# Splitting the product S4 B22 of a tile pair into seven quarter products in matrices four to seven of a relational graph layer

## The chip, the cores and the metric

The kernel runs on one core of one Trainium2 chip. The metric is the device time of one execution in microseconds (us); the kernel before took 1364.59, 1365.10 and 1367.09 us in three runs, a median of 1365.1 us. The profile is of one further execution.

A core has five engines that run side by side, each in the order of its own instructions, and wait for each other by semaphores: TensorE (PE in the profile, its weight loads PEld), VectorE (DVE), ScalarE (ACT), GpSimd (POOL) and SyncE (SP, which here only issues transfers). TensorE writes to PSUM, eight banks of 128 partitions x 512 fp32 values; DVE and ACT read them.

## The reference

All arrays are fp32. N = 1250 nodes, D = 1024 features, R = 8 relations, E = 20000 edges sorted by destination.

```
h = relu(layernorm(x))
u = h @ root + bias
for r in range(8):
    sums = segment_sum(h[src] * (edge_type == r), dst)       # one row for each node
    u   += (sums / max(count of such edges, 1)) @ weight[r]
z   = concat([u, x']) @ w_gate + b_gate                      # x' is the layer's input, h
out = x + tanh(u) * z + h * (1 - z)
```

## The kernel before

**Order of the arithmetic.** The kernel multiplies first and gathers afterwards: y_r = h @ weight[r] for every relation, then for each node the weighted sum of rows of y. So there are eleven matrices of 1024 x 1024 (`NM`): eight relations (numbers 0 to 7), the root (8) and the two halves of w_gate (9 and 10). `step(s, i, ...)` multiplies matrix s by row tiles i and i + 5 (2 x 128 rows) of h. Ten row tiles make five steps i = 0 to 4 a matrix.

**One step.** `product` takes the two row tiles as the upper and lower half of a left matrix, halves it in columns too, and halves the right matrix both ways (blocks of 512 x 512). It forms the result by Winograd's variant of Strassen's scheme: seven products of blocks where eight would be needed. The left sums S1 to S4 are kept for all matrices in `h_op`, the right sums T1 to T4 (`make_t1` and so on) are made by DVE for each matrix. Every block product is four matmuls of 128 x 512 (`add`). The order is A11, S1 (T1), S2 (T2), S3 (T3), S4 (B22), A22 (T4), with A12 (B21) apart; two banks, b and c, collect sums. ACT copies partial results into the output rows (lines 331, 338, 342, 360) or into a tile `part` (317), and DVE adds the rest (310, 318, 326). After each block product `done()` calls `between(j)`, j = 0 to 6, where work for DVE, POOL and the queues is put in.

**Pairs.** In matrices 1 to 9 the steps (0, 1) and (2, 3) are pairs (`paired`). Their two products A12 B21, which share the right block, are taken together, by the same scheme one level lower: class `Second` makes seven products of quarters, each of two matmuls of 128 x 256 (line 213). They are hung between the block products of the two steps by the dictionary `fill`, under the names "first" to "fourth" of the place after which they stand. The result row `to` of the even step's first tile is kept until the odd step has added its share (lines 240, 241, 244), and is then stored (`put(i - 1, 0, to)`); the odd step's share is added in lines 247, 248 and 251.

**PSUM.** Six of the eight banks rotate under the name `ps` (`bank()`); two more, `ps_n` and `ps_q`, have one buffer each and serve the index work in matrices 0 to 3. A tile's next use waits until the readers of the one before are through.

**Edges.** The index work of the first matrices sorts edges into slots for each node. From matrix 4 on, `edges(g, ...)` gathers rows of y by POOL transfers into four buffers `got` (line 1065), and DVE adds each, scaled, to a sum `u` (lines 1071, 1073): group 0 beside matrices 4 and 5, group 1 beside 6 and 7, group 2 beside 8 and 9. `spread` deals these out over the calls of `between`, about one gather a block product. Matrix 10 and the gate come last. Everything is ordered by hand (`manual_schedule`): the text of the program is the order on each engine.

**Other names that the change touches.** `key_col`, `row_col` and `rank` hold three columns of numbers for the edges; they are kept to the end, because a branch for overlong edge lists (`tc.If(passes > 0)`), which this input doesn't take, reads them again. `bias_bc` is the bias spread over the partitions (read at line 398 from matrix 8 on), `t_w` and `far_k` are small scratch tiles of the edge weights and of `passes_needed`.

Of the kernel before, what the change touches and what calls it, by code (L numbers as in the profile page):

```python
# [19 lines left out]
def tile_rgcn_highway(  # L20
# [95 lines left out]
    table_more = dram.tile([G * KEYS * MORE, 1], I32, name="table_more")  # L116
    val_dram = dram.tile([G, KEYS], F32, name="val_dram")
# [134 lines left out]

    def transposed(aop, part, of, n, relu=False):


        for half, to in enumerate(((A11, A12), (A21, A22))[part]):
            p = bank().rearrange("p (k f) -> p k f", k=KQ)
            for i in range(KQ):
                k = KQ * half + i
                nc.tensor.transpose(p[:, i, :n], of[:n, k * P:(k + 1) * P], ident[:n, :n])  # L260
            to_n, p_n = aop[:, to, :, :n], p[:, :, :n]
            if half and relu:
                nc.vector.tensor_scalar_max(to_n, p_n, 0.0)
            elif half:
                nc.vector.tensor_copy(to_n, p_n)
            else:
                nc.scalar.activation(to_n, p_n, AF.Relu if relu else AF.Copy)
            if n < P:
                nc.gpsimd.memset(aop[:, to, :, n:], 0.0)
# [9 lines left out]
    def product(aop, w, to, between=lambda j: None, last=None, pieces=1, whole=True,  # L279
                fill=None, second=None, third=None):  # L280
# [48 lines left out]
        b, c = bank(), bank()  # L329
# [15 lines left out]
        if whole and not third:  # L345
            p3()
            d = p7()
            if not second:
                p2()
        else:  # L350
            d = p7()
            if third:
                last(d, 0)
            p3()
# [26 lines left out]
    waiting = {}  # L381

    def step(s, i, between=lambda j: None, second=None):
# [21 lines left out]
        def beside(j):  # L405
# [3 lines left out]
            if two and i == 0:  # L409
                sums(j)  # L410
            if two and (i, j) == (1, 6):
                Second(fac[s], 2).left()
# [26 lines left out]
        fill = {}  # L439
        if two:  # L440
            e, to = waiting[i - i % 2]
            if i == 0:
                fill = dict(sixth=lambda: (e.second(), e.second_to_first(to)))
            elif i == 1:
                fill = dict(first=lambda: e.first(),
                            fifth=lambda: (e.sixth(), True),
                            sixth=lambda: (e.seventh(), e.to_first(to), 0)[-1],
                            seventh=lambda: (e.fourth(), e.to_second(t[0]), put(i - 1, 0, to),
                                             0)[-1],
# [6 lines left out]
            else:  # L456
                fill = dict(first=lambda: (e.to_second(t[0]), e.fourth_to_second(t[0]), 0)[-1],
                            sixth=lambda: (e.second(), True),
                            seventh=lambda: (e.second_to_first(to), put(i - 1, 0, to), 0)[-1])
        product(h_op[i], fac[s], t, between=beside, whole=not two, fill=fill, second=second)  # L460
# [13 lines left out]
    key_col = const.tile([P, NCH], F32, name="key_col")  # L474
    row_col = const.tile([P, NCH], I32, name="row_col")
    rank = const.tile([P, NCH], F32, name="rank")
# [70 lines left out]
    with ExitStack() as early:  # L547
# [148 lines left out]
        tb_col = ix1.tile([P, NCH], F32, name="tb_col")  # L696
        less_lo = ix1.tile([P, NCH], F32, name="less_lo")
# [319 lines left out]
        def index():  # L1017
            for _ in zip_longest(norms(), columns()):
                yield
            with tc.tile_pool(name="ix", bufs=2) as ix:  # L1020
                yield from slots(ix)
            yield from order()
# [17 lines left out]
    with ExitStack() as edges_part:  # L1040
        gpool = edges_part.enter_context(tc.tile_pool(name="gpool", bufs=GOT))
        upool = edges_part.enter_context(tc.tile_pool(name="upool", bufs=UB))
        bias_bc = edges_part.enter_context(tc.tile_pool(name="bpool", bufs=1)).tile(
            [P, D], F32, name="bias_bc")
        nc.sync.dma_start(bias_bc, bias[None, :].to_broadcast([P, D]))
        small = edges_part.enter_context(tc.tile_pool(name="small", bufs=1))
        t_w = small.tile([P, ND, SLOTS], F32, name="t_w")
        drc = small.tile([P, ND], F32, name="drc")

        def weights(g):  # L1050
            slot_weights(g, idx[:, g, :, :SLOTS], w_of[:, g], t_w, drc)
# [3 lines left out]
        def got():  # L1055
# [4 lines left out]
            return t  # L1060

# [71 lines left out]
        def passes_needed():  # L1133

            far_k = small.tile([P, NHI], F32, name="far_k")
# [72 lines left out]
        with tc.If(passes > 0):  # L1208
# [22 lines left out]
            done = rank  # L1231
            nc.vector.tensor_single_scalar(done, rank, float(-SLOTS), op=OP.add)
# [30 lines left out]

        LG = G - 1
# [186 lines left out]
```

## Time and profile before

| what | value |
|---|---|
| three runs, us | 1364.59, 1365.10, 1367.09 |
| the profiled execution, us | 1364.05 |
| its span from first to last instruction, us | 1362.3 |
| mean granted TensorE clock | 0.999 |
| matmul records of 128 x 512 (line 293) | 2784, mean 594 ns with overlap |
| matmul records of 128 x 256 (line 213) | 504, mean 380 ns with overlap |
| DVE waiting for gathers, matrices 4 to 7, us | 103.4 |
| POOL waiting for DVE, matrices 4 to 7, us | 120.7 |
| HBM read and written, MB | 214.20 and 80.65 |

How to read it: busy time of an engine is the union of its instructions; for PE, whose matmuls overlap, the mean of one is longer than its share of the time. A row of the timeline gives start, duration, engine, line of the kernel, operation, output <- inputs, shape and count; in square brackets stand the idle time of the engine before it and what ended that. A fp32 matmul of the program leaves two records on PE. Line numbers are those of the kernel before.

### The profile page before, as it was taken

How to read it: one execution, taken by the hardware profiler on the slowest of the kernel's cores; microseconds unless marked ns; L12 is line 12 of the kernel's file. 1: busy time of each engine (PE TensorE's matmuls, PEld its weight loads, DVE VectorE, ACT ScalarE, POOL GpSimd, SP SyncE). 2: the span in 40 equal slices, each digit the busy share in tenths (PEclk: the TensorE clock that was granted, in tenths of full speed). 3: DMA queues.
4: the chain of work that ended last, by engine and by line, in shares of the span. 5: the costliest groups of instructions: out<-in, count | busy, mean ns of one | idle time of the engine just before them, and what ended most of it. 6: DMA issues, size and time to landing. Idle time of an engine off the chain costs nothing.

```text
span 1362.3 us, 12814 instructions
## 1 busy us (share of the span) xinstructions
PE 1350.3 (99%) x3810; PEld 659.9 (48%) x3810; DVE 932.0 (68%) x1849; ACT 365.4 (27%) x792; POOL 639.8 (47%) x571
## 2 busy tenths in 40 slices
PE   9999999999999999999999999999999999999998
PEld 5444445455445544544554454455445445544443
DVE  7855976887884976557565746865564585568975
ACT  3235656565641111111111111111111111121220
POOL 0001655665553358657774435465443243435631
PEclk9999999999999999999999999999999999999999
DMA  8744665944663258479788628787965764587851
GB/s 308 271 182 145 95 138 141 212 85 118 158 181 95 49 172 183 109 272 225 227 286 318 223 72 294 263 289 272 342 222 195 235 226 153 190 285 244 287 188 58
DMA packets 110218, 272.77 MB, mean 200 GB/s; under 512 B 25972, under 2 KB 28002, under 8 KB 110016
## 3 DMA queue, kind: packets, MB, share of 16 engines
q0 software_dynamic: 48912, 128.60, 29.7%
q1 hardware_dynamic: 45104, 111.34, 27.2%
q10 hardware_dynamic: 16128, 31.98, 7.6%
q8 instruction: 30, 0.49, 0.2%
q14 instruction: 44, 0.36, 0.1%
HBM read 214.20 MB, written 80.65 MB: 216 GB/s over the span
## 4 chain that ended last, share of the span: by engine, by line
PE 90%; issue 4%; DVE 2%; DMA 2%; POOL 1%; SPq 1%; ACT 0%; POOLq 0%; DVEq 0%; ACTq 0%
PE ps L293 80%; PE ps L213 8%; DMA xt<-in_x_dram 1%; PE ps L260 1%; DMA w<-in_L_gnn_weight_dram 1%; PE ps_n L805 1%; POOL out_dram L497 1%; SPq L561 0%; PE ps_q L856 0%; DVE u L1276 0%; POOL got L491 0%; DVE h_op L276 0%; DVE row L1377 0%; DVE h_op L1323 0%; DVE h_op L1340 0%
## 5 line engine op out<-in xcount | busy, mean ns | idle before, releaser
L293 PE MATMUL ps<-w,h_op 128*128 128x512 f32 x2800 | 1224.4, 593 | 2.0 <-ACT row L342 1.0
L293 PEld LDWEIGHTS ps<-w,h_op 128*128 128x128 f32 x2800 | 526.5, 190 | 615.6 <-issue 600.6
L1065 POOL DMA_INDIRECT got<-y,idx x202 | 259.8, 1286 | 243.7 <-DVE u L1073 189.6
L1073 DVE SCALAR_TENSOR_TENSOR u<-got,w_of,u 128x1024 f32<-128x1024 f32 (+1 forms) x192 | 245.9, 1282 | 137.6 <-DMA got<-y,idx 135.4
L884 POOL DMA_INDIRECT table<-row_col,at_i x157 | 176.6, 1125 | 160.9 <-DVE at_i L880 74.5
L318 DVE TENSOR_TENSOR row<-row,part 128x512 f32<-128x512 f32 x55 | 37.9, 689 | 103.6 <-ACT part L317 99.8
L360 ACT COPY row<-ps 128x512 f32<-128x512 f32 x50 | 29.3, 585 | 240.5 <-PE ps L293 236.6
L317 ACT COPY part<-ps 128x512 f32<-128x512 f32 x55 | 32.2, 586 | 178.3 <-PE ps L293 164.4
L310 DVE TENSOR_TENSOR row<-row,ps 128x512 f32<-128x512 f32 x54 | 36.9, 684 | 62.3 <-PE ps L293 50.1
L331 ACT COPY row<-ps 128x512 f32<-128x512 f32 x55 | 32.2, 585 | 165.3 <-PE ps L293 154.7
L338 ACT COPY row<-ps 128x512 f32<-128x512 f32 x55 | 32.2, 586 | 146.2 <-PE ps L293 131.4
L213 PE MATMUL ps<-w,w 128*128 128x256 f32 x288 | 71.3, 380 | 0.0
L342 ACT COPY row<-ps 128x512 f32<-128x512 f32 x55 | 32.2, 586 | 139.0 <-PE ps L293 133.3
L213 PEld LDWEIGHTS ps<-w,w 128*128 128x128 f32 x288 | 54.4, 190 | 20.9 <-issue 15.3
L528 POOL DMA_INDIRECT node_dram<-ids,pos_i x30 | 40.1, 1336 | 45.4 <-issue 45.4
L870 DVE SCALAR_TENSOR_TENSOR junk<-k_bc,key_col,before 128x128 f32<-128x128 int32 x157 | 54.9, 350 | 4.2
L810 DVE TENSOR_TENSOR seen<-seen,ps_n 128x110 f32<-128x110 f32 x157 | 42.1, 268 | 21.1 <-PE ps_n L805 11.8
L213 PE MATMUL ps<-w,h_op 128*128 128x256 f32 x216 | 56.0, 382 | 0.0
L213 PEld LDWEIGHTS ps<-w,h_op 128*128 128x128 f32 x216 | 40.5, 190 | 25.6 <-issue 22.1
L787 ACT ACTIVATE is_lo<-io,less_lo 128x128 bf16<-128x128 f32 x157 | 50.1, 391 | 0.7 <-DMA xh_dram<-xt 0.7
L938 DVE SCALAR_TENSOR_TENSOR junk<-v_bc,val,one 128x1280 bf16<-128x1280 f32 x30 | 46.5, 1550 | 0.8
L491 POOL DMA_INDIRECT u<-u_dram,node x20 | 22.5, 1126 | 51.3 <-DMA last_dram<-u 35.0
(187 smaller groups left out, 957.7 us busy)
## 6 DMA issues: line engine op xcount, KB each, us to landing
y<-row SPq DMA_DIRECT2D x72, 512.0 KB
w<-in_L_gnn_weight_dram ACTq DMA_DIRECT2D x21, 1024.0 KB
w<-in_L_gnn_weight_dram SPq DMA_DIRECT2D x10, 1024.0 KB
k_bc<-keys_dram SPq DMA_DIRECT2D x39, 256.0 KB
l_bc<-los_dram SPq DMA_DIRECT2D x39, 256.0 KB
w<-in_L_gnn_w_gate_dram ACTq DMA_DIRECT2D x6, 1024.0 KB
h_dram<-h_op SPq DMA_DIRECT2D x9, 512.0 KB
hr_dram<-row SPq DMA_DIRECT2D x9, 512.0 KB
```

The lines of the kernel that those rows point to most:

```text
L213: nc.tensor.matmul(p, a[:, k, :], b[:, k, :], start=(fresh and k == 0), stop=(k == 1), skip_group_check=True)
L293: nc.tensor.matmul(b[:, at], aop[:, i, k, :], w.of[i][:, k, at], start=(fresh and k == 0), stop=(k == KQ - 1), skip_group_check=True)
L310: nc.vector.tensor_add(c12, c12, c)
L318: nc.vector.tensor_add(c22, c22, d)
L528: ins = nc.gpsimd.indirect_dma_start(out=node_dram[g][:, :], out_offset=bass.IndirectOffsetOnAxis(ap=pos_i[:, g, d:d + 1], axis=0), in_=id ...
L787: nc.scalar.activation(is_lo[:, i, :], io, AF.Abs, bias=less_lo[:, c0 + i:c0 + i + 1])
L810: nc.vector.tensor_add(seen[j][:, i, :], was, p[:, i, :])
L870: nc.vector.scalar_tensor_tensor(junk, o["k_bc"][:, i, :], key_col[:, c:c + 1], before, op0=OP.is_equal, op1=OP.mult, accum_out=rank[:, c: ...
L884: ins = nc.gpsimd.indirect_dma_start(out=table[:, :], out_offset=bass.IndirectOffsetOnAxis(ap=at_i[:n, i:i + 1], axis=0), in_=row_col[:n, ...
L938: nc.vector.scalar_tensor_tensor(junk, v_bc[:, g, :], val[:, c:c + 1], one.to_broadcast([P, KEYS]), op0=OP.is_gt, op1=OP.mult, accum_out=p ...
L1065: nc.gpsimd.indirect_dma_start(out=t[:n], out_offset=None, in_=y[g][:, :], in_offset=bass.IndirectOffsetOnAxis(ap=at[:n, d, k:k + 1], axis=0),
L1073: nc.vector.scalar_tensor_tensor(u[:n], t[:n], w, u[:n], op0=OP.mult, op1=OP.add)
```

## The change

In matrices 4 to 7 (`thirds(s)`: R0[1] < s < ROOT, with R0[1] = 3 and ROOT = 8) the two products S4 B22 of a pair are also taken together as seven products of quarters, in a new class `Third`. Its sums s1, s2, t1, t2 are made in two goes in four small tiles (`room`), the second go (`next_sums`) writing over the first. Three of the seven products are added to what already stands in PSUM: in the even step bank c, which holds S1 T1, is now the tile `ps_n` (`hold`) and is kept until the odd step; the odd step's c and the tile `ps_q` take the others. The odd step's "first" place gets three quarter products (`first`), the place of S4 B22 gets one in the even step (`second`) and three in the odd one (`last`). The row `to` is stored after `last_to`, no longer at the place "seventh".

To make room in memory, the three edge columns move to the index pool and are written to DRAM by three transfers on SP between `slots` and `order`, the untaken branch reads them back, `t_w` and `far_k` become gather buffers, and `bias_bc` is loaded after the branch instead of at the start of the edge part.

```diff
+    edges_dram = dram.tile([3, P, NCH], F32, name="edges_dram")
...
+    class Third:
+        def __init__(self, f, i, room):
+            b = f.place["b22"]
+            self.b11, self.b12, self.b21, self.b22 = [
+                b[:, k:k + 2, c:c + H] for k in (0, 2) for c in (0, H)]
+            self.a11, self.a12, self.a21, self.a22 = [
+                h_op[i + o][:, S4, k:k + 2] for o in (0, 1) for k in (0, 2)]
+            self.t1, self.t2, self.s1, self.s2 = room
+        def sums(self):
+            nc.vector.tensor_add(self.s1, self.a21, self.a22)
+            nc.vector.tensor_sub(self.t1, self.b12, self.b11)
+            nc.vector.tensor_sub(self.s2, self.s1, self.a11)
+            nc.vector.tensor_sub(self.t2, self.b22, self.t1)
+        def next_sums(self):
+            nc.vector.tensor_sub(self.s1, self.a11, self.a21)
+            nc.vector.tensor_sub(self.t1, self.b22, self.b12)
+            nc.vector.tensor_sub(self.s2, self.a12, self.s2)
+            nc.vector.tensor_sub(self.t2, self.b21, self.t2)
+        def hold(self):
+            self.c0 = psum.tile([P, CG, P], F32, name="ps_n", bufs=1).rearrange("p c k -> p (c k)")
+            return self.c0
+        def second(self, c):
+            Second.add(self, c[:, :H], self.a12, self.b21)
+        def first(self):
+            self.b = psum.tile([P, 512], F32, name="ps_q", bufs=1)[:, :H]
+            self.c = bank()[:, :H]
+            self.p = rows.tile([P, Q], F32, name="part", bufs=2)
+            Second.add(self, self.b, self.a11, self.b11, True)
+            nc.scalar.copy(self.p[:, :H], self.b)
+            Second.add(self, self.c, self.s1, self.t1, True)
+            Second.add(self, self.b, self.s2, self.t2)
+            nc.scalar.copy(self.p[:, H:], self.b)
+        def last(self, c):
+            Second.add(self, self.b, self.s1, self.t1)
+            Second.add(self, self.c0[:, H:], self.s2, self.b22)
+            Second.add(self, c[:, :H], self.a22, self.t2)
+        def first_to(self, to):
+            nc.vector.tensor_add(to, to, self.p)
+            nc.vector.tensor_add(to[:, H:], to[:, H:], self.c)
+        def fifth_to(self, to):
+            nc.vector.tensor_add(to[:, H:], to[:, H:], self.c)
+        def last_to(self, to, to1, c):
+            nc.vector.tensor_add(to, to, self.c0)
+            nc.vector.tensor_add(to1, to1, c)
+            nc.vector.tensor_add(to1.rearrange("p (a n) -> p a n", a=2),
+                                 to1.rearrange("p (a n) -> p a n", a=2),
+                                 self.b[:, None, :].to_broadcast([P, 2, H]))
...
-        b, c = bank(), bank()
+        b = bank()
+        c = inner.hold() if inner and inner.holds else bank()
...
-            p3()
+            if inner:
+                inner.then(c)
+                done()
+                filled("third")
+            else:
+                p3()
...
+    def thirds(s):
+        return R0[1] < s < ROOT
...
+            if q and i % 2 == 0 and j == 1:
+                q.sums()
+            if q and i % 2 and j == 1:
+                q.next_sums()
+                q.first_to(to[:, Q:])
+            if q and i % 2 and j == 4:
+                q.fifth_to(t[0][:, Q:])
...
+                def then(c):
+                    if q.holds:
+                        q.second(c)
+                    else:
+                        q.last(c)
+                        q.last_to(to[:, Q:], t[0][:, Q:], c)
+                        put(i - 1, 0, to)
...
-                fill = dict(first=lambda: e.first(),
+                fill = dict(first=lambda: (e.first(), q and q.first(), 0)[-1],
...
-                            seventh=lambda: (e.fourth(), e.to_second(t[0]), put(i - 1, 0, to),
-                                             0)[-1],
+                            seventh=lambda: (e.fourth(), e.to_second(t[0]),
+                                             q or put(i - 1, 0, to), 0)[-1],
...
-                fill = dict(first=lambda: (e.to_second(t[0]), e.fourth_to_second(t[0]), 0)[-1],
+                fill = dict(first=lambda: (e.to_second(t[0]), e.fourth_to_second(t[0]),
+                                           q and q.first(), 0)[-1],
...
+            for k, t in enumerate((key_col, row_col.bitcast(F32), rank)):
+                nc.sync.dma_start(edges_dram[k], t)
             yield from order()
...
-        bias_bc = edges_part.enter_context(tc.tile_pool(name="bpool", bufs=1)).tile(
-            [P, D], F32, name="bias_bc")
-        nc.sync.dma_start(bias_bc, bias[None, :].to_broadcast([P, D]))
...
+        inner_pool = inner_part.enter_context(tc.tile_pool(name="inner", bufs=1))
+        room = [inner_pool.tile([P, 2, n], F32, name=f"inner{k}")
+                for k, n in enumerate((H, H, P, P))]
...
+            t_w = got()[:, :ND * SLOTS].rearrange("p (d k) -> p d k", k=SLOTS)
...
-            far_k = small.tile([P, NHI], F32, name="far_k")
+            far_k = got()[:, :NHI]
...
+        inner_part.close()
+        bias_bc = edges_part.enter_context(tc.tile_pool(name="bpool", bufs=1)).tile(
+            [P, D], F32, name="bias_bc")
+        nc.sync.dma_start(bias_bc, bias[None, :].to_broadcast([P, D]))
```

## The prediction

> **What bounds the kernel now.** I read three views in this order. First the page's table of engines:
>
> ```profile
> PE 1350.3 (99%) x3810; PEld 659.9 (48%) x3810; DVE 932.0 (68%) x1849; ACT 365.4 (27%) x792; POOL 639.8 (47%) x571
> ```
>
> TensorE (PE) is busy for 1350.3 of 1362.3 us. A busy PE need not be a PE at its peak, and an average says nothing of the stage that is changed. So second, the busy time by stretches; each is one matrix long (four, five, six and seven), cut where the last product of the matrix before ends:
>
> ```profile
> 514.20:633.00 118.80, 118.80 (x306) 57.54 (x305) 67.24 (x85) 17.63 (x33) 81.26 (x72) 1.00 0.76 203
> 633.00:751.70 118.70, 118.70 (x305) 57.48 (x304) 77.55 (x88) 17.63 (x33) 75.51 (x68) 1.00 0.82 261
> 751.70:870.70 119.00, 119.00 (x307) 57.60 (x306) 74.01 (x111) 17.63 (x33) 53.46 (x47) 1.00 0.63 223
> 870.70:989.40 118.70, 118.70 (x305) 57.51 (x304) 76.73 (x80) 17.63 (x33) 63.92 (x58) 1.00 0.80 280
> ```
>
> After the stretch and its length come PE, weight load, VectorE (DVE), ScalarE (ACT), GpSimd (POOL), granted clock, DMA share. PE equals the length in all four, at clock 1.00: matmul records set the time, and a record less or shorter counts in full. DVE is idle for 41 to 52 us of each. The list of waits over these stretches says what for: 103.4 us in all on gathers (DMA got<-y), 39.4 on ACT's part, 16.6 on PE. Third, what one record costs. PE in order of time, in matrix five, tile pair 1:
>
> ```profile
> 657.94 1.03 PE L213 MATMUL ps<-w,h_op 128*128 128x256 f32 x4
> 658.81 1.03 PE L213 MATMUL ps<-w,w 128*128 128x256 f32 x4
> 659.67 3.60 PE L293 MATMUL ps<-w,h_op 128*128 128x512 f32 x8
> 663.10 1.89 PE L213 MATMUL ps<-w,w 128*128 128x256 f32 x8
> 664.83 3.60 PE L293 MATMUL ps<-w,h_op 128*128 128x512 f32 x8
> 668.26 1.03 PE L213 MATMUL ps<-w,w 128*128 128x256 f32 x4
> 669.13 3.67 PE L293 MATMUL ps<-w,h_op 128*128 128x512 f32 x8
> 672.64 1.03 PE L213 MATMUL ps<-w,h_op 128*128 128x256 f32 x4
> ```
>
> A product of four matmuls leaves eight records, two for each. The second column holds the tail that overlaps the next line, so the price is the distance of the starts: 663.10 - 659.67 = 3.43 us for 8 wide records, 0.429 each; 664.83 - 663.10 = 1.73 for 8 narrow ones, 0.216 each.
>
> **The part on PE.** In each of two pairs of four matrices the two S4 products (2 x 4 matmuls, 16 wide records) go: 16 x 0.429 = 6.86 us. Seven quarter products of two matmuls come, 28 narrow records: 28 x 0.21625 = 6.06 us. That is 0.80 a pair, and **6.4 us** over eight pairs.
>
> A rule that speaks against it: the Trainium skill, "TensorE: Matmul & The Clock Gate", section "Back-to-back issue gap", has a stream of weight loads and matmuls sustain 81 ns a matmul at 128 columns and 131 ns at 512. On a straight line that is an estimated 98 ns at 256, so 0.75 of the wide price. By it 28 records would cost 28 x 0.75 x 0.429 = 9.0 us, a loss of 2.1 a pair and 17 us in all. The rows above give 0.50, because the load (190 ns in the groups by shape) fits under a 216 ns record. The row decides; twenty narrow records in a row, which the change makes, are not in the trace, but the x8 line has no slope within it.
>
> **New cover problem on ACT.** In an even product the S3 result in b is copied by ACT (L317), and the last product adds onto b afterwards. The S4 product lay between, 3.43 us; in the pair's even product now two quarter matmuls, 0.86 us. That case is in the trace: at 668.26 four narrow records stand between S2 and the S3 that needs the copy L342. PE then takes 672.64 - 668.26 = 4.38 us where 0.86 + 3.43 = 4.29 would do, 0.09 lost. It recurs in product 0 of each matrix (product 2 keeps four more matmuls there): 4 x 0.09 = **0.4 us** lost. In first(), b is rewritten after 0.86 us too, but its copy is a 256-wide one of 0.37 us (L219) that starts 0.2 us after its records end, 0.29 us before it is needed: 0.
>
> **DVE.** Per pair, from the rows: sums and next_sums each 2 x 0.69 (as L203) + 2 x 0.42 (as L206 to L209) = 2.22; first_to 0.69 + 0.42; fifth_to 0.42; last_to 3 x 0.68 (as L310); less two L310. 4.44 + 1.11 + 0.42 + 2.04 - 1.36 = 6.65 us a pair, 13.3 a matrix. The last addition of last_to reads a 256-wide bank twice over, for which there is no row: between 0.41 (256 elements written) and 2 x 0.41; L310 has its written size, so 0.68. DVE goes from 67-78 to 81-91 us of 117: not the bound, and hidden in the mean by those waits for gathers. What counts is being late. DVE runs strictly in order, and here it is late already, in matrix five, behind a gather:
>
> ```profile
> 677.17 1.28 DVE L1073 SCALAR_TENSOR_TENSOR u<-got,w_of,u 128x1024 f32<-128x1024 f32 x1 [5.51 <-DMA got<-y,idx]
> 678.37 0.68 DVE L240 TENSOR_TENSOR row<-row,w 128x512 f32<-128x512 f32 x1
> 679.16 0.42 DVE L241 TENSOR_TENSOR row<-row,ps 128x256 f32<-128x256 f32 x1
> 679.50 0.69 DVE L318 TENSOR_TENSOR row<-row,part 128x512 f32<-128x512 f32 x1
> 680.10 1.28 DVE L1073 SCALAR_TENSOR_TENSOR u<-got,w_of,u 128x1024 f32<-128x1024 f32 x1
> 681.29 0.42 DVE L247 TENSOR_TENSOR row<-row,w 128x256 f32<-128x256 f32 x1
> 681.75 0.42 DVE L248 TENSOR_TENSOR row<-row,w 128x256 f32<-128x256 f32 x1
> 682.09 0.68 DVE L310 TENSOR_TENSOR row<-row,ps 128x512 f32<-128x512 f32 x1
> ```
>
> The S4 product that L310 adds ended at about 676.9 on PE, so DVE is 5.2 us behind. Until now nobody waited: its bank came back six banks later. After the change that place holds last_to, and its first addition frees c0, the single ps_n bank, which product 2 needs for S1. So the **new wait** is PE's, for DVE, two products after last(). Behind it stands the whole PE stream. Worked out: the gather that lands at 677.17 was issued at 672.80 by POOL, which was held up by its own idx and node gathers and did not wait for DVE; so next_sums, first_to and sums disappear in the waits before it (4.3, 5.5 us and five of about 0.8 us in this pair). Behind it only fifth_to is new, 0.34 to the next start: the first addition runs 682.43 to 683.11. S1 of product 2 starts at 683.80 now; it comes earlier by 1.5 (matrix four) and 0.7 (this pair), at 681.6. PE would stand for 1.5 us.
>
> It may be more. The gathers may come later, for POOL waits for DVE to free a buffer (120.7 us here), and the Trainium skill, "GPSIMD Engine Reference", section "Specifications", says that GpSimd's SBUF interfaces contend with DVE instructions that have two SBUF inputs; 5 of the 6.65 us are of that kind. The row L1065 runs from 984 to 5668 ns, median 1013, mean 1286, so issues do stretch, though the row does not say why. By the median alone 1.5 stands; if the two sums (4.4 us) were half pushed into the gather it would be near 4. It may be nothing, if the gather lands 1.6 us sooner. I take **2 us**, near the row, with ends 0 and 4. Matrix four has 2.5 us to spare by the same sum (L310 at 560.79, S1 of product 2 at 565.05); in six and seven L310 waits for PE, so DVE is not behind there. The second pair's c0 has product 4 in between: no wait.
>
> **What costs nothing, and its cover.** PE's wait for next_sums: they stand at product 1's second step, four PE stages (about 7 us or more) before last(); without that cover, DVE's lag would be paid here first. The even tile's row store moves from the fourth quarter product to behind last_to; SP then holds this pair's other stores behind it, and ACT's copy into that row (S1 of product 2) would wait, about 10 us after last() ends; a late copy would delay S3 some 5 us further on. ACT gets two 0.37 us copies a pair in an engine busy 18 of 119. The edge columns go out by three SP issues (0.3 to 0.4 us each, as L912) at about 426 us, ahead of val_dram, v_bc, the rc stores and y stores: up to 1.2 us on a queue whose readers come steps later. The bias load moves from 515 us to behind the register read at 990.7 on SP; its first reader is L398 at 1012.5, 21 us of cover. t_w and far_k take gather buffers: one POOL memset (0.98) ahead of the first gather, at 508 us, whose reader comes at 522. The edges_dram reads on POOL lie in the branch that isn't taken.
>
> **Sum.** -6.4 + 0.4 + 2.0 = -4.0 us. On the profiled execution (span 1362.3, whole 1364.05, so 1.75 around it) that is 1360.0; the median of the runs stands 1.05 above it, so 1365.1 - 4.0 = **1361.1**.
>
> **Rivals.** (A) Likeliest, 0.45: one stand in matrix five, 1360.0 to 1362.3. (B) All is hidden, 0.25: DVE's idle 41 us speak for it, the 5.2 us lag against; 1365.1 - 6.0 = 1359.1. (C) The change doesn't do what it says in time, 0.17: stands in several first pairs, say 1.4 us in each of four matrices, eat the gain: -6.0 + 5.6 gives 1364.7. Against it is L310's wait for PE in six and seven. (D) Slower, 0.13: the ps_n handover, after the first pair of every matrix. If the added 13.3 us push gathers and lag together so that each first pair stands as at matrix five's upper end, 4 us: 16 - 6 = +10, 1375. It decides from 2.2 us a matrix on (8.7 in all). For it: POOL and DVE wait for each other already; against it: DVE idles a third of each matrix.
>
> **Range and chances.** A measurement of this kernel can tell about 0.2% (2.7 us) from no change. B starts at 1358.6 with a little room for the rows' rounding; C reaches 1367.5, and only D's upper part and a strip of C lie outside: 1358.6 to 1367. A's own range is 1360.0 to 1362.3. Faster (under 1362.4): A and B, less a little for A's upper end: 0.68. Same: C and that bit: 0.18. Slower: D and C's end: 0.14.
>
> **What would show it.** L293's wide records fall by 8 x 16 = 128 and narrow L213 ones rise by 8 x 28 = 224. Right: matrices four, six and seven some 1.5 us shorter, five less, with a PE wait for DVE before the S1 of its product 2. Wrong: runs of narrow records at more than 0.22 us each (the rule), PE waits for s1 or t1 at last(), a stand in every matrix (D), or ACT standing for a row store.

## The result, and the profile after

The changed kernel takes 1359.91 us (median of 22 runs, 1358.51 to 1367.83); the kernel before, beside it, 1365.20 us (22 runs, 1364.29 to 1367.09). The ratio is 0.9967, with a 95% interval of 0.9959 to 0.9975: faster by 4.5 us, between 3.4 and 5.6. The ratio is one of means; the medians lie 5.3 us apart. Eighteen of the 22 runs lie from 1358.5 to 1361.7, with a median of 1359.4, four from 1364.2 to 1367.8; that tail comes up again below. The profiled execution took 1361.69 us, the longest of the eighteen; it has a span of 1359.9 us at a granted clock of 0.999.

The page's table of engines, after:

```profile
PE 1344.6 (99%) x3906; PEld 677.5 (50%) x3906; DVE 976.3 (72%) x1945; ACT 371.3 (27%) x808; POOL 648.9 (48%) x571
```

PE has 96 records more (224 narrow ones come, 128 wide ones go) and 5.7 us less of busy time. The stretches of matrices four to seven, after, cut as before:

```profile
515.80:633.00 117.20, 117.20 (x330) 61.98 (x329) 78.02 (x109) 19.09 (x37) 81.25 (x71) 1.00 0.71 195
633.00:752.40 119.40, 117.43 (x329) 61.89 (x328) 88.78 (x112) 19.10 (x37) 80.58 (x69) 1.00 0.85 264
752.40:869.80 117.40, 117.40 (x331) 62.08 (x330) 85.32 (x135) 19.09 (x37) 56.12 (x47) 1.00 0.65 227
869.80:987.00 117.20, 117.20 (x329) 61.98 (x328) 87.71 (x104) 19.10 (x37) 64.14 (x58) 1.00 0.82 284
```

Three matrices are 1.5 to 1.6 us shorter than before and PE is busy all through them. Matrix five is 0.7 us longer, and its PE column is 1.97 us short of its length: one wait. The list of waits, after, names it first:

```profile
PE ps_n L356 <- DVE row L309: 2.0, 1, 2.0
```

And in order of time, matrix five, PE:

```profile
672.76 1.03 PE L214 MATMUL ps<-w,h_op 128*128 128x256 f32 x4
673.62 1.03 PE L214 MATMUL ps_q<-inner,inner 128*128 128x256 f32 x4
674.49 1.03 PE L214 MATMUL ps_n<-w,inner 128*128 128x256 f32 x4
675.35 1.03 PE L214 MATMUL ps<-inner,h_op 128*128 128x256 f32 x4
676.22 7.03 PE L356 MATMUL ps<-w,h_op 128*128 128x512 f32 x16
685.22 3.70 PE L356 MATMUL ps_n<-w,h_op 128*128 128x512 f32 x8 [1.97 <-DVE row L309]
```

Lines 673.62 to 675.35 are `last()`: four narrow records each 0.865 us from the next, 0.216 a record, as priced. (Twenty in a row stand from 655.48 to 659.79 us, again 0.216 each.) Then come 16 wide ones, and S1 of product 2 stands 1.97 us for the single `ps_n` bank. DVE in the same window:

```profile
679.23 1.28 DVE L1175 SCALAR_TENSOR_TENSOR u<-got,w_of,u 128x1024 f32<-128x1024 f32 x1 [2.82 <-DMA got<-y,idx]
...
682.16 0.41 DVE L306 TENSOR_TENSOR row<-row,ps 128x256 f32<-128x256 f32 x1
...
684.48 0.68 DVE L309 TENSOR_TENSOR row<-row,ps_n 128x512 f32<-128x512 f32 x1
```

The gather that held DVE landed at 679.23, 2.06 us later than before, when matrix four had begun 1.6 us later; behind it `fifth_to` (L306) and `last_to` (L309) follow in order.

Below, a matrix's length is the distance between the starts of ACT's last copy at line 429 (the last copy of a step) in two successive matrices. Before: 118.76, 118.76, 118.98, 118.76 for matrices four to seven. After: 117.19, 119.43, 117.41, 117.20, a sum 4.03 less.

### The profile page after: what moved, and what is told of

The parts are those of the page before. It is cut to its first block, busy times and chain, and to the rows that moved or that the text cites. A ratio compares the mean times of both kernels' runs of the same rounds, so it can differ in the third digit from the quotient of the medians.

```text
span 1359.9 us, 13144 instructions
## 1 busy us (share of the span) xinstructions
PE 1344.6 (99%) x3906; PEld 677.5 (50%) x3906; DVE 976.3 (72%) x1945; ACT 371.3 (27%) x808; POOL 648.9 (48%) x571
## 4 chain that ended last, share of the span: by engine, by line
PE 45%; DMA 6%; issue 5%; DVE 4%; POOL 2%; POOLq 0%; DVEq 0%
PE ps L356 37%; DMA got<-y,idx 5%; PE ps L214 5%; PE ps_n L356 1%; DVE u L1175 1%; PE ps_q L214 1%; POOL got L1167 1%; DMA node_dram<-ids,pos_i 1%; PE ps_n L214 1%; POOL out_dram L593 1%; PE ps L322 0%; DVE w L204 0%; POOL idx L587 0%; DVE w L181 0%; POOL got L587 0%
## 5 line engine op out<-in xcount | busy, mean ns | idle before, releaser
L356 PE MATMUL ps<-w,h_op 128*128 128x512 f32 x2608 | 1145.1, 593 | 3.0 <-issue 1.2
L356 PEld LDWEIGHTS ps<-w,h_op 128*128 128x128 f32 x2608 | 489.7, 190 | 568.8 <-issue 553.4
L1167 POOL DMA_INDIRECT got<-y,idx x202 | 264.8, 1311 | 231.7 <-DVE u L1175 173.7
L429 ACT COPY row<-ps 128x512 f32<-128x512 f32 x50 | 29.2, 584 | 222.6 <-PE ps L356 204.9
L395 ACT COPY row<-ps 128x512 f32<-128x512 f32 x55 | 32.1, 585 | 163.0 <-PE ps L356 149.7
L406 ACT COPY row<-ps 128x512 f32<-128x512 f32 x55 | 32.2, 585 | 138.6 <-PE ps L356 132.1
L402 ACT COPY row<-ps 128x512 f32<-128x512 f32 x47 | 27.5, 585 | 127.9 <-PE ps L356 106.9
L373 DVE TENSOR_TENSOR row<-row,ps 128x512 f32<-128x512 f32 x38 | 26.0, 685 | 44.8 <-PE ps L356 29.8
L214 PEld LDWEIGHTS ps<-w,h_op 128*128 128x128 f32 x216 | 40.5, 190 | 25.6 <-issue 22.3
```

Of the source, the lines that this page charges most:

```text
L214: nc.tensor.matmul(p, a[:, k, :], b[:, k, :], start=(fresh and k == 0), stop=(k == 1), skip_group_check=True)
L356: nc.tensor.matmul(b[:, at], aop[:, i, k, :], w.of[i][:, k, at], start=(fresh and k == 0), stop=(k == KQ - 1), skip_group_check=True)
L1167: nc.gpsimd.indirect_dma_start(out=t[:n], out_offset=None, in_=y[g][:, :], in_offset=bass.IndirectOffsetOnAxis(ap=at[:n, d, k:k + 1], axis=0),
```

## The experiments

The theory on trial at the outset: PE gains 1.57 us a matrix, DVE's new work is hidden, the moves of buffers and transfers cost nothing, and matrix five loses 2.2 us because DVE comes late from a gather and TensorE needs the single bank. Its rivals: the moves or DVE's work cost time by themselves; the stand comes from the sums that the change puts on DVE; the lateness has other ways to TensorE than that bank.

The experiments ran in four batches, each on another chip, and the kernel before has another median in each (1361.8 to 1365.9 us). So each ratio is taken against the runs of before in the same batch, and within a profile the lengths of matrices are compared. The first four matrices drift too: matrix four starts at 511.9 to 519.1 us over the profiles, at 514.27 in the one of before, 512.82 in a second one, 515.86 in the one of after. The last column of the table is from one profiled execution of each kernel, which need not be a usual one: that of `no_sums` (1366.81 us) is the longest of its twelve, those of `second_pairs` (1366.19) and `five_first_pair` (1366.42) are 3 us above their medians.

| kernel | us, median (lowest to highest, runs) | ratio to before (95%) | matrices four to seven, us |
|---|---|---|---|
| the change | 1359.91 (1358.51 to 1367.83, 22) | 0.9967 (0.9959 to 0.9975) | 117.19, 119.43, 117.41, 117.20 |
| moves_only | 1364.62 (1363.59 to 1368.74, 11) | 1.0008 (1.0000 to 1.0017) | 118.76, 118.76, 118.98, 118.76 |
| dve_only | 1367.90 (1363.71 to 1375.41, 11) | 1.0030 (1.0011 to 1.0048) | 118.76, 118.76, 118.98, 118.76 |
| no_sums | 1360.82 (1358.23 to 1366.81, 12) | 0.9979 (0.9969 to 0.9989) | 117.19, 123.91, 117.41, 117.19 |
| act_c0 | 1368.47 (1366.70 to 1369.89, 5) | 1.0033 (1.0020 to 1.0046) | 117.19, 124.35, 117.41, 117.20 |
| second_pairs | 1363.17 (1358.41 to 1367.24, 12) | 1.0000 (0.9987 to 1.0013) | 117.93, 124.57, 118.15, 117.94 |
| skip_five | 1358.59 (1357.12 to 1360.75, 7) | 0.9969 (0.9959 to 0.9980) | 117.19, 118.76, 117.41, 117.19 |
| later_group | 1364.34 (1361.91 to 1371.50, 12) | 1.0015 (1.0003 to 1.0028) | 118.42, 117.19, 123.16, 117.42 |
| spread_groups | 1369.60 (1368.31 to 1371.97, 5) | 1.0055 (1.0041 to 1.0069) | 117.19, 117.19, 124.35, 117.41 |
| five_first_pair | 1363.33 (1360.13 to 1371.52, 12) | 0.9984 (0.9967 to 1.0001) | 117.90, 122.30, 117.41, 117.19 |
| before_again | 1362.60 (1) | | 118.76, 118.76, 118.98, 118.76 |
| dve_again | 1361.75 (1) | | 118.76, 118.81, 118.98, 118.76 |
| after_again | 1362.79 (1) | | 117.19, 123.68, 117.41, 117.19 |

### The moves alone, and the kernel before once more

`moves_only` keeps every move of buffers and transfers and takes the new products nowhere:

```diff
     def thirds(s):
-        return R0[1] < s < ROOT
+        return False
```

> All moves of the change (edge columns by way of DRAM, t_w and far_k in gather buffers, bias loaded later, the four room tiles) and none of the quarter products. Theory (they are hidden): the time of before within 0.1%, 1364 to 1366.5. Rival (the 1.6 us by which matrices 0 to 3 ended later in the profile of the changed kernel come from the moves): 1366.7, and the start of matrix four in the profile at 515.9 us instead of 514.3.

> The kernel before, profiled once more. If the first four matrices vary by themselves, matrix four starts 1.5 us or more away from the 514.3 us of the first profile; if the moves of the change cost what the profiles with them show (start at 515.9 to 519.1), it starts at 513.8 to 514.8 again, and matrices four to seven take 118.8 each.

The ratio is 1.0008, and the four matrices have their old lengths to 0.01 us. But matrix four starts at 516.76 us in this profile, even later than the rival said. The start varies with the batch, though, and this batch has no profile of before. In the batch that has one (512.82 us), two kernels with all the moves, `skip_five` and `second_pairs` below, start matrix four at 512.41 and 512.99. So the moves cost nothing that these runs can tell (up to 0.0017 of the time, 2.3 us, is within the interval), and the 1.6 us by which matrix four starts later in the profile of after is most likely drift.

### DVE's work alone

`dve_only` takes TensorE's products as before and keeps additions of the same shapes beside them on DVE, into tiles that nothing reads:

```diff
...
+            if inner and not inner.holds:
+                nc.vector.tensor_add(inner.t2, inner.t2, inner.t2)
+            p3()
...
-                q.first_to(to[:, Q:])
+                nc.vector.tensor_add(q.s1, q.s1, q.s1)
+                nc.vector.tensor_add(q.t1, q.t1, q.t1)
...
-                q.fifth_to(t[0][:, Q:])
+                nc.vector.tensor_add(q.s2, q.s2, q.s2)
```

> The kernel with both S4 products as before on PE, but with DVE's added work: sums and next_sums as they are, first_to, fifth_to and the net of last_to as additions of the room tiles onto themselves (6.6 us a pair, 53 us in all); the result doesn't use them. Theory (DVE's load is hidden by its waits for gathers as long as nobody on PE waits for last_to): the time of before within 0.1%, 1364 to 1366.5. Rival (the load itself puts off the gathers and with them PE, as in the forecast's slower case): 1367 or more, with PE waits in matrices four to seven.

> The kernel of dve_only once more, for a second look at where its time goes (before's products on TensorE, with VectorE's additions of the change put beside them; they add into nothing that is used elsewhere or double it, so the output is another). If the excess of dve_only over moves_only (3 us) was a wait in the first matrices that came by chance, matrices four to seven are 118.8 us each again and the wait is elsewhere or gone; if VectorE's work costs time by itself, one of the four matrices is 120 us or more.

In both profiles the four matrices are as before to 0.05 us: with TensorE at its old pace DVE's extra work reaches nobody. Yet the runs of `dve_only` are about 4 us above before. Its profiled execution (1369.0 us) shows one wait of 2.57 us, in matrix two, ahead of all that was changed; `dve_again` shows none and takes 1361.75 us beside a before of 1361.76. The profiles don't hold an explanation of the runs' median, which stays open; what they show is that DVE's work alone needs no wait of TensorE in these matrices, not that it never costs one. (No tile of the result is touched, so the output is that of before, and not another, as the second expectation has it.)

### The sums left out

`no_sums` leaves out both `sums` and `next_sums`, so the products that use s1, s2, t1 and t2 are taken of zeros, and the output is another:

```diff
             if q and i % 2 == 0 and j == 1:
-                q.sums()
+                pass
             if q and i % 2 and j == 1:
-                q.next_sums()
...
+        for r in room:
+            nc.vector.memset(r, 0.0)
```

> The changed kernel without sums and next_sums (the four room tiles are set to zero once, so three of the seven products of a pair and what follows from them are left out of the result's value; all PE and ACT instructions stay). It takes 4.4 of the 6.65 us of DVE work a pair away. Theory (the sums hide in DVE's waits for gathers; the stand in matrix five is only the gather's lateness plus fifth_to): PE still waits 1 to 2.2 us for last_to in matrix five, time as the changed kernel less at most 1 us, 1359 to 1360. Rival (the added DVE work makes the stand): no wait of PE for DVE, 1358.0.

If DVE's load made the stand, it had to shrink. The waits of PE in this kernel:

```profile
PE ps_n L356 <- DVE row L309: 4.0, 1, 4.0
```

It is twice as long. DVE, ahead of it, had waited 4.37 us for a gather that landed at 681.86, 2.6 us later than in the change. So the stand needs no sums; it follows the gather. Nor do the runs gain by leaving the sums out (0.9979, where the change has 0.9967). The length of matrix five, 123.91, is 6.7 us above that of matrix four, more than a wait of 4.0. PE in stretches cut where the clock changes, in the columns length, PE busy (records), granted clock, DMA share and GB/s:

```profile
682.65:686.07 3.42, 1.24 (x3) 1.00 0.20 54
686.07:689.48 3.41, 1.63 (x2) 0.50 0.78 231
689.48:692.89 3.41, 3.41 (x5) 0.50 0.84 266
692.89:696.31 3.42, 3.42 (x9) 1.00 1.00 364
```

From 686.07 us, still within the wait, the clock is at half for 6.83 us. The Trainium skill, "TensorE: Matmul & The Clock Gate", section "What's actually happening", has such a gate: a free-running window of 3413 ns, and half clock after an idle window. The trace's 6.83 us are two of these windows. A stand of 1.97 us (in the change) lost no clock; this one of 3.96 us did, though no window of it was idle throughout. The last section comes back to this.

### The bank freed early

`act_c0` lets ACT copy what stands in the single bank to a tile as soon as `last()` has added its product there, and DVE add from that tile:

```diff
             Second.add(self, self.c0[:, H:], self.s2, self.b22)
+            self.p0 = rows.tile([P, Q], F32, name="part", bufs=2)
+            nc.scalar.copy(self.p0, self.c0)
             Second.add(self, c[:, :H], self.a22, self.t2)
...
-            nc.vector.tensor_add(to, to, self.c0)
+            nc.vector.tensor_add(to, to, self.p0)
```

> ACT copies the bank c0 into a part tile right after last(), and DVE adds from there; nothing else differs from the changed kernel. Theory (PE's stand in matrix five is the handover of the single ps_n bank through a late DVE): ACT frees the bank about 0.8 us after last(), the 2.0 us wait is gone, matrix five takes 117.2 us like four, six and seven instead of 119.4, and the profiled span falls by 2.0 to 2.2; the median about 1358.5, and the long executions of the changed kernel (1364 to 1368) go too, if they are the same wait grown longer. Rival (PE stood for the gathers or for DVE's load in general): another wait of about 2 us takes its place in matrix five.

The stand at the bank is gone: S1 of product 2 starts at 683.21 with no wait. But the kernel is slower than before. Matrix five takes 124.35 us, with a new wait in the second pair. ACT and PE there:

```profile
741.39 0.58 ACT L404 COPY row<-ps 128x512 f32<-128x512 f32 x1 [10.89 <-DMA y<-row]
```

```profile
742.03 18.96 PE L358 MATMUL ps<-w,h_op 128*128 128x512 f32 x40 [5.29 <-ACT row L404]
```

ACT's copy of product 4 goes into the row buffer whose store SP issued behind `last_to`, at 733.07, and stands until it has landed, 8.3 us later; PE stands for ACT. The prediction had this store at nothing. What cover it had is read from SP's issues and ACT's copy into that row in order of time, before and then after:

```profile
725.21 3.61 SPq L403 DMA_DIRECT2D y<-row  x3
...
734.76 0.59 ACT L338 COPY row<-ps 128x512 f32<-128x512 f32 x1 [2.80 <-PE ps L293]
```

```profile
729.32 2.98 SPq L476 DMA_DIRECT2D y<-row  x3
...
735.46 0.58 ACT L402 COPY row<-ps 128x512 f32<-128x512 f32 x1 [2.80 <-PE ps L356]
```

From issue to copy it was 9.6 us before and is 6.1 in the change, where the copy still waits for PE alone. The step behind `last_to` used up a third of the cover, and in `act_c0` the store was issued some 4 us later still. In the first pair the cover is shorter: in the change SP issued that store at 685.19, and ACT's copy, due at about 688.9, did wait for it, without a wait of PE:

```profile
689.84 0.58 ACT L402 COPY row<-ps_n 128x512 f32<-128x512 f32 x1 [5.93 <-DMA y<-row]
```

### Only the second pairs

Is that second way there without the first? `second_pairs` takes the new form in the pairs (2, 3) alone:

```diff
-            if thirds(s):
+            if thirds(s) and i >= 2:
```

> The changed kernel with the quarter products for the tile pairs (2, 3) only, in all four matrices. Their c0 is taken again a whole product later. Theory: 4 x 0.80 us less on PE, no wait for last_to, 0.6 lost to the moves: ratio 0.9975 to 0.9985, matrices of 118.0 us. Rival (in this pair the late row store, as with the copy of c0 by ACT, holds PE in matrix five): matrix five longer than 118.5 us with a wait of PE for ACT.

It is. The waits of PE in this kernel, and the ACT copy in order of time:

```profile
PE ps L356 <- ACT row L402: 4.7, 1, 4.7
```

```profile
739.26 0.59 ACT L402 COPY row<-ps 128x512 f32<-128x512 f32 x1 [10.23 <-DMA y<-row]
```

SP issued the stores from 729.46, almost as in the change, but this one landed 9.8 us later, where in the change 6.1 us were enough. The DMA queues are full (share 1.00 from 732 to 736 us in both). The 12 runs fall into two groups of six, 1358.4 to 1361.1 and 1365.2 to 1367.2. That the long group are executions with this wait is likely, as the profiled one (span 1364.4) is of that kind, but no profile of a short one was taken.

### All but matrix five

```diff
     def thirds(s):
-        return R0[1] < s < ROOT
+        return R0[1] < s < ROOT and s != 5
```

> The changed kernel with the quarter products in matrices four, six and seven only. Theory: 3 x 1.57 us less on PE, no stand, about 0.6 us lost to the moves: ratio 0.9965 to 0.9975, and no executions far above the median. Rival (the stand comes from the change as a whole, and another matrix takes it over): a wait of PE of 2 us or more in matrix six or seven, ratio 0.998 or above.

With matrix five left as it was, PE waits for nothing in these four matrices, no run lies over 1360.75 us, and the ratio is that of the change, 0.9969 against 0.9967. The new form brings three times 1.57 us in the other matrices and, within the intervals, nothing in five: what it saves there, the stands take back.

### The crowd on the queue moved

Beside matrix five POOL also issues the node and index transfers of group 2 (`other_groups`, line 624 in the change), between the gathers. `later_group` puts them beside matrices six and seven; `spread_groups` deals those of groups 1 and 2 out over two matrices each:

```diff
-        def other_groups():
-            for g in range(1, G):
+        def other_groups(groups):
+            for g in groups:
...
-            others = other_groups()
+            others = other_groups((1,))
...
+        def group_two_first():
+            for _ in other_groups((2,)):
+                yield
+                yield
+            yield from passes_needed()
...
-            passes = passes_needed()
+            passes = group_two_first()
```

(`spread_groups`: four yields a step instead of two, group 1 at every fourth step, and 10 yields instead of 30 in `passes_needed`.)

> The changed kernel, but the node and idx transfers and the weights of edge group 2 are dealt out beside matrices six and seven instead of five; the work itself is the same. Theory (in matrix five POOL's node and idx transfers hold up the gathers, DVE is late behind them, and PE then stands for c0 or a row store): no PE wait of over 1 us in matrix five, which takes 117.2 us; the long executions go, and the time is 1365.2 - 6.2 + about 0.6 for the moves, 0.9955 to 0.9965 of before. Rival (DVE's own load makes it late, or the gathers' bandwidth): matrix five keeps a wait of 2 us or more, or a new one comes in six or seven where POOL has more to do; ratio 0.997 or above.

> The change, with the nodes and indices of groups 1 and 2 dealt out at every fourth step over two matrices each instead of in one crowd. Theory (matrix five is paced by gathers that the crowded transfers of group 2 hold up; what is late there reaches TensorE): with the crowd spread, TensorE waits for nothing over 1 us in matrices four to seven, matrices four, five, six and seven take 117.2 to 117.8 us each, the ratio is 0.9955 to 0.9965 and no execution lies 4 us above the median. Rival (the slack for the gathers is too short by itself; spreading only moves the stand): TensorE waits 2 us or more in one of the four matrices, and the ratio is 0.998 or more.

In both, matrix five takes 117.19 us, without a wait, where all six profiles with the new form and the crowd in matrix five have one: what was theory of the place is right. But the stand comes up in matrix six instead, so each kernel's ratio follows its rival (the change's loss is moved, not removed). PE in `later_group`, and in `spread_groups`:

```profile
795.22 1.17 PE L214 MATMUL ps_q<-inner,inner 128*128 128x256 f32 x4 [4.01 <-DVE inner L275]
```

```profile
801.67 5.40 PE L356 MATMUL ps_n<-w,h_op 128*128 128x512 f32 x8 [3.94 <-DVE row L309]
```

The first is a third way: `next_sums`, which had been taken as covered by four PE stages, stands behind two gathers, and `last()` waits for it. Behind both the clock halves again. Moving the transfers moves the stand; POOL issues the gathers and its other transfers in one order, and where both meet, DVE falls behind. (In `later_group` S1 also stands 0.96 us at the bank in matrix four.) In `spread_groups` a further 7 us go after all work: its last POOL transfer ends at 1357.8 us as in `after_again` (1358.0), but the engines' closing barrier puts the span's end at 1367.8 instead of 1361.0. What delays it isn't known, so this kernel's ratio says little of the theory; its matrices do.

### The change once more

> The change once more, for a second profile. Theory: matrices four, six and seven 117.2 to 117.5 us; matrix five 118 to 120 us with one wait of TensorE of 1 to 2.5 us and no halved clock, or, in a long execution, a wait of 2.5 us or more with the clock halved behind it and 123 us or more. Rival (matrix five's loss was particular to the first profile): matrix five 117.2 to 117.5 us like the others.

Matrices four, six and seven repeat to 0.01 us. Matrix five does not: no wait at the single bank this time, but 1.44 us for a load of weights at its start, and in the second pair the wait of the row store. The waits of PE:

```profile
PE ps L356 <- ACT row L402: 3.1, 1, 3.1
PE ps L214 <- DMA w<-in_L_gnn_weight_dram: 1.4, 1, 1.4
```

The clock halves for 3.41 us from 737.88 on:

```profile
734.00:738.00 4.00, 1.07 (x3) 0.99 1.01 393
738.00:742.00 4.00, 3.85 (x6) 0.59 1.01 407
```

So the change itself has executions in which the store decides, and in this one it gains nothing: the four matrices sum to 475.47 us, 0.2 more than before. It takes 1362.79 us where before, in the same batch, has a median of 1361.76: 1.0 us more. The four long runs of the change lie from 1.0 us below to 2.6 us above their median of before, so it is of their size; that those four are of this kind was not seen in a profile.

### Both ways closed

The last run closes both: in matrix five only the first pair is new, with ACT's copy out of the bank.

```diff
-            if thirds(s):
+            if thirds(s) and (s != 5 or i < 2):
...
                 q.holds = i % 2 == 0
+                q.copied = s == 5
...
+            self.p0 = self.c0
+            if self.copied:
+                self.p0 = rows.tile([P, Q], F32, name="part", bufs=2)
+                nc.scalar.copy(self.p0, self.c0)
```

> The change, but in matrix five only the first pair takes the new form, and there ScalarE copies the first quarter-row of products out of the single bank (as in act_c0); the second pair of matrix five stays as before. Theory (matrix five is paced by late gathers; the lateness reaches TensorE in the first pair over the single bank and in the second pair over the late store of a row; with both roads closed it reaches TensorE nowhere): matrices four, six and seven 117.2 to 117.4 us, matrix five 118.0 to 118.4 us without a wait of 1 us, no execution 4 us above the median, ratio 0.995 to 0.997. Rival (the lateness is passed on to a further wait, the store of the first pair's row among them): a wait of 2 us or more in matrix five, ratio 0.998 or more.

The rival holds again. DVE, at the start of matrix five, and PE:

```profile
640.00 1.28 DVE L1180 SCALAR_TENSOR_TENSOR u<-got,w_of,u 128x1024 f32<-128x1024 f32 x1 [6.90 <-DMA got<-y,idx]
641.20 0.68 DVE L385 TENSOR_TENSOR row<-row,part 128x512 f32<-128x512 f32 x1
641.80 2.29 DVE L173 TENSOR_TENSOR w<-w,w 128x2048 f32<-128x2048 f32 x1
```

```profile
644.23 5.17 PE L360 MATMUL ps<-w,h_op 128*128 128x512 f32 x8 [2.44 <-DVE w L173]
```

A fourth way, through work that the change does not touch: DVE waits 6.90 us for a gather, and T1 of matrix five (L173) comes 2.44 us late. Eight wide records then take 5.17 us where 3.60 is their row, because the clock is at half from 643.84 to 647.25. (Matrix four, which has the change's form here, takes 117.90, with a wait of 0.45 at the bank.) Neither profile of before has a wait over 1 us in these four matrices. No kernel tried beats the change beyond the intervals; `skip_five` has its ratio without its tail.

## Why the prediction was right

**The time.** 1361.1 us was forecast, 1359.9 came, 0.1 us below the likeliest case's own range, and the ratio's 4.5 us (3.4 to 5.6) holds the forecast 4.0. The profiled execution has the mechanism of that case (A): one stand, in matrix five, at S1 of product 2, and -4.03 us over the four matrices against -4.0. The span fell by only 2.4, because the first four matrices took 1.6 us longer in that execution. Part of this is luck. The profiled execution is the longest of the eighteen short ones. Their median is 5.8 us below before, which is nearer to case B, where all is hidden (6.0), than to A; no profile of a shorter one was taken. The second profile of the change has another stand and no gain. So the median may be a mixture of B and of a tail, and whether A's stand is in the usual execution stays open.

**PE's records.** -128 wide, +224 narrow, as counted, at 0.216 us also in a row of twenty. The rule that would have made it three quarters of the wide price fell: it would have cost 17 us.

**ACT's copy.** Mis-sized: 0.10 us a matrix was forecast, but 1.57 of PE's 1.60 us arrive, so it costs 0.03 (0.1 in all, not 0.4).

**DVE's work.** 13.3 us a matrix forecast, 11.1 measured in busy time (78.0 to 88.8 a matrix, where 81 to 91 was forecast). The forecast summed durations, but in a row the next addition starts before the one ahead has ended: a 512-wide one of 0.69 us is followed after 0.60 (679.50 to 680.10 in the prediction's rows), a 256-wide one of 0.42 after 0.34. With these distances the same sum is 11.3. `last_to`'s last addition was put at 0.68 and takes 0.69. The work is hidden in both profiles of it alone, where the four matrices keep their lengths; the runs of that kernel, 1.0030 of before, stay unexplained.

**The stand of 2 us.** Right in size for the profiled execution, 1.97, and by luck. The row gave 1.5 and half a microsecond was added. Then both ends moved: the gather landed 2.06 us later than in the profile of before, and S1 was due at 683.25 (685.22 less the wait), 1.65 later than the 681.6 worked out, because matrix four began later; the 0.4 between them is about what had been added. The row of before fixed neither: in the five profiles with the new form in this pair and without ACT's copy, the stand at this bank was 1.97 (the change), 0 (`after_again`), 3.96 (`no_sums`), and 0 twice where the crowd was moved. The doubt named for it, that the sums push the gathers, was not borne out: without the sums it was 3.96. Matrix five's loss is 2.24 us against its gain of 1.57, so a little more than the wait goes. Matrix four, put at 2.5 us to spare, had 0.3: `last_to`'s first addition ends at 565.61 and S1 starts at 565.89. In `later_group` and `five_first_pair` S1 stood there, 0.96 and 0.45 us.

**The row store at nothing** is the step that failed. The 10 us of cover were counted from the end of `last()` on TensorE. But the store is issued only behind `last_to`'s first addition on DVE, which the prediction's own figures put at 683.11, some 8 us after `last()`. From issue to copy it was 6.1 us in the second pair of the change, and in the first pair 3.7 to the time when the copy was due, which then stood 0.9 us for the store. A store on the full queues took 8.3 to 9.8 us in the second pair where the copy had to wait for it. It was the larger wait in the second profile of the change (3.08 us). Priced rightly, it would have been a chance of +5 to +7 us (3.08 to 5.29 of wait, and the clock): in size that fits the four long runs, 4 to 8 us above the median.

**`next_sums` covered by four stages.** True in the change; false when the crowd of transfers stands in the same matrix (`later_group`, 4.01 us).

**A term that was missing.** A stand was priced at its length. In these four matrices each stand of 2.44 us or more cost 1.7 us or more on top, because the clock halved (last section).

**The moves at nothing.** Right as far as `moves_only` (at most 2.3 us by its interval) and `skip_five` can tell.

## What to carry to other kernels

When work is taken off the engine that sets the time, price what is left of the slack of the engines that feed it, not only the work: here each matrix comes 1.57 us sooner, the gather that paces matrix five did not, and where one way by which its lateness arrived was closed, another showed, four in all. A store that is moved later is a load on the buffer it reads: measure issue to next write of that buffer in the profile of before, and take off what the move adds. Where a cover is counted from one engine's work and what it covers starts on another, add that engine's lag. If one stage has no slack, leaving it as it was (`skip_five`) can be worth as much as the change there, with less spread.

## What was unexpected of the hardware

How sharply a short stand of TensorE turns into lost clock, and that its length is not what decides. In all fourteen profiles every change of the granted clock lies on one grid of 3.4133 us that runs through the whole execution: in `after_again`, for one, the changes are at 7.43, 737.88, 741.30 and 1359.11 us, which are 214, 1 and 181 times 3.4133 us apart. (In the change itself they are at 5.40 and 1357.08, 396 times.) So each wait can be cut where the grid cuts it:

| wait of PE, us | kernel | PE idle in each window of the grid, us | half clock, us |
|---|---|---|---|
| 1.97 | the change | 1.41, 0.56 | 0 |
| 2.01 | later_group, matrix two | 0.40, 1.61 | 0 |
| 2.44 | five_first_pair | 2.05, 0.39 | 3.41 |
| 2.57 | dve_only, matrix two | 0.18, 2.39 | 3.41 |
| 3.08 | after_again | 2.82, 0.26 | 3.41 |
| 3.94 | spread_groups | 0.59, 3.35 | 3.41 |
| 3.96 | no_sums | 2.17, 1.79 | 6.83 |
| 4.01 | later_group | 1.57, 2.45 | 3.41 |
| 4.67 | second_pairs | 1.65, 3.02 | 3.41 |
| 5.29 | act_c0 | 1.57, 3.41, 0.30 | 3.41 |

A window at full clock in which PE was idle for 1.65 us or less was followed by a window at full clock, one with 2.05 us or more by a window at half clock. The 1.79 us of `no_sums` fell in a window that was at half clock already, and the next was at half clock too. No window of these profiles from the first rise of the clock on breaks this. The limit lies between 1.65 and 2.05 us, so it may be half a window (1.71), which these runs don't settle; the ends of matmuls are modelled, so the idle times are not exact. The page quoted above halves the clock after a whole idle window; of the nine windows in the table that were followed by half clock, one was idle throughout.

What a stand costs is thus in part luck: how the grid lies over it. By these limits a wait of 2.05 us can halve the clock, and one of up to 3.3 us (an estimate, twice 1.65) may not. One window at half clock costs 1.7 to 2.0 us beyond the wait: in `later_group` matrix six takes 123.16 us, 5.75 more than without a wait (117.41), and 4.01 of them are the wait; in `five_first_pair` matrix five takes 122.30, where one new pair without a wait would be 118.76 - 0.79 = 117.97, and 2.44 of the 4.33 lost are the wait.
